# A hand-pipelined four-layer graph kernel: another order of all steps, on all engines

## The chip, the core and the metric

The kernel runs on one core of a Trainium2 chip. The core's engines work side by side: PE (TensorE, matrix products and transposes), DVE (VectorE), ACT (ScalarE), POOL (GpSimd), and SP, whose queue issues the DMA transfers. Each takes its own instructions strictly in the order in which the program gives them; an instruction whose input isn't there holds up everything behind it on its engine. The metric is the device time of one execution in microseconds (us), the median of several runs.

## What is computed

128 samples `x` of 128 nodes by 512 features, float32, go through four layers. `adj` (128 by 128) is shared by all samples. Each layer ends in `x = layernorm(x + layer(x))`.

```
layer 0:  deg = adj.sum(1);  nadj = adj * rsqrt(deg)[:,None] * rsqrt(deg)[None,:]
          nadj @ (x @ W0) + bias
layer 1:  max_j relu(A[:, j] + (C - A)[:, i]) with W1 = W2 = adj
layer 2:  q, k, v = x @ Wq.T, x @ Wk.T, x @ Wv.T
          rel = adj.T * (q @ k.T);  rel = rel / norm(rel, axis=2);  rel @ v
layer 3:  h = x @ W3;  e = leaky_relu((h @ a1)[:,None] + (h @ a2)[None,:]) * adj
          att = softmax(e);  elu(att @ h + beta * h)
```

Layer 1 adds to each row only a multiple of what the normalisation removes again, so the kernel keeps of it a factor in the variance.

## The kernel before, in words

**Tiling.** The samples are taken in 32 groups of 4; a group's `x` is one tile of 128 by 4 by 512. A program step is one small piece of one group's work, such as one product block, one copy out of PSUM, or one exchange; it is written `group.step`, as `0.w5`. Steps of the setup, common to all groups, are `s.step`.

**Order.** Three strings list the steps: HEAD (setup and the first groups), TURN (the steady state, one group per turn, with steps of five neighbouring groups mixed) and TAIL (the last groups). In TURN and TAIL the group number is relative to a base. A loop at the end of the kernel goes through HEAD, then TURN once for each group from FIRST to NG + LAST, then TAIL; `BACK` is taken off to get the base. Under `manual_schedule` the order of the steps is the order on each engine's queue. No planner intervenes afterwards. FIRST is 5 and LAST −6, so TURN is run 21 times. In TAIL the base is 22, and `9.` is the last group, 31.

**The stages of a group**, with the step names that matter here:

- `ld` loads x (`load`, L286). The loads of groups 0 to 3 and of all weights are issued once in the setup (L286, L333 to L351), in the order adj, x_0 (two halves), x_1, W0, bias, Wq, Wk, Wv, W3, a, beta, x_2, x_3.
- Layer 0: `y10 … y11` multiply nadj with x (`aggregate`, L736), ACT copies the result out of PSUM (`cy`, `copy` L375). `w1 … w7` is the product with W0 as seven blocks of Strassen's scheme (L565). Block 2 is cut again into small products (`w2`, `w28`; L529) for most groups. The left operand's sums `sy0 … sy3` run on POOL (`pool_tt`, L381). `dw`, `tw`, `uw` add the blocks into x (DVE L378, ACT L375, POOL L381), `bi` adds the bias (POOL). Then `stw` (`stats`, L770), `vaw` (L782), `pow` (POOL, L384), `nbw` (L790) and `apw` (ACT, L796) are the layernorm.
- Layer 2: `xt` transposes x on DVE in 32 by 32 blocks (`square`, L459) and `xd` completes the transposition with 16 DMAs on SP (`exchange`, L465). `sx0 … sx3` (POOL) are sums of the result, `lx1`, `lx2` sums for small blocks. `z` (with gq = Wk and Wq folded into one matrix), `r0 … r3` (`pe_r`, L905), `rm` (mask), `sq`, `rp` (norm), `rt`/`wr`/`cr` (the transposition of rel through DRAM, L497 and L501), `v` (the product with wvT) and `f`/`fa` (rel times v, L953, added on DVE at L963) follow, and the layernorm with `v`.
- Layer 3: `sc` (the two scores of every sample, DVE, L972, with `wa_bc` = W3·a spread over the partitions), `pw`/`pe` (the second score through DRAM; for the last group four PE transposes `ps`, L896), `pl`, `ej`, `ei`, `ex`, `rd`, `so` (mask and softmax), `at`/`aw`/`cat` (att transposed through DRAM; for the last group by PE, `pat`), `nt`/`nd` (x transposed and exchanged, as above), `k` (product with W3), `h` (att times it), `em`, `ee`, `ea` (elu; L1061, L1064, L1068), the layernorm with `k`, and `fin` (output DMA, L805). The last group's product is a plain one (`k_plain`, L827; half columns in `jk`, L869 to L891).

**The setup.** `s.g1 … s.g7` is the product gq (seven blocks, bank by bank), with `cg`, `dg`, `tg`, `ug` putting it together; its sums of Wq are `s.sa0 … s.sa3` on POOL, of Wk `s.sk`. `s.vt` and `s.vd` transpose and exchange Wv (16 DMAs on SP), `s.sv` are its sums. Eight `s.q` (DVE, L662) form wa = W3·a. `s.wd` (SP, L675) writes it to DRAM as `d_wa`, `s.wb` (L679) reads it back into all partitions as `a_bc`. `s.wc0` and `s.wc1` (ACT, L375) copy it to two PSUM banks kept for it. `wb` waits for `wd`, `wc` for `wb`.

**Buffers.** PSUM: 6 banks in a ring (tag "bank") and the two of `wa_bc`. Left operands aT and their sums S have 3 buffers each, most others one. The tile `q` of the small blocks, allocated in `before`, has one buffer.

Of the kernel before, what the change touches and what calls it, by code (L numbers as in the profile page):

```python
# [50 lines left out]
FIRST = 5  # L51
LAST = -6
BACK = 4
HEAD = """
s.warm s.deg s.root s.nadj s.adjt s.nadjT 0.ld 0.y10 0.y00 0.cy10 0.y11 0.cy00 0.sy1 1.ld 0.y01
0.cy11 1.y10 0.cy01 0.sy0 1.y00 1.cy10 0.sy2 1.y11 1.cy00 1.y01 1.cy11 s.s00 0.sy3 0.w1 1.cy01
s.s02 0.w5 s.s01 0.dw1 0.bi01 0.w7 0.dw5 s.sa0 s.s03 0.w2 0.dw7 s.sa1 0.w6 s.sk0 0.dw2 s.sa2
0.w3 0.tw s.sk2 s.sk1 0.w4 s.m02 0.dw3 s.sa3 s.g1 0.dw4 0.bi00 s.g2 s.cg1 s.sk3 s.vt0 0.bi10
s.g5 s.vt1 0.bi11 s.dg2 s.vt2 s.g7 s.cg5 0.uw01 s.vt3 2.ld 3.ld s.vd s.q00 s.g6 s.dg7 0.uw10
0.stw0 0.uw11 s.g3 0.stw1 s.q01 s.tg s.g4 0.stw2 1.sy0 0.stw3 1.sy1 1.w1 s.dg3 0.vaw 1.sy2 s.dg4  # L60
1.w5 1.dw1 0.pow s.q02 1.w7 0.nbw 1.dw5 1.ly2 0.apw0 0.apw1 1.dw7 0.apw2 s.q03 1.w2 0.apw3 s.q10
1.w6 1.bw2 0.xt0 1.sy3 1.ew2 s.ug11 1.w3 0.xt1 1.bi10 1.tw 0.xt2 1.w28 0.xt3 1.w4 1.bi00 0.xd
s.sg0 2.y10 s.sv0 2.y00 s.sg2 2.cy10 s.sg1 2.y11 2.cy00 s.sv2 2.cy11 s.sg3 s.sv1 1.dw3 1.bi11
1.dw2 2.y01 1.bi01 1.dw4 2.cy01 s.sv3 s.q11 s.q12 s.q13 s.s30 s.wd s.bi 1.uw01 0.z1 s.s32 1.stw0
0.sx0 0.cz1 1.stw1 0.sx1 0.z5 s.wb s.mg1 0.z2 0.cz5 s.s31 0.sx2 0.z7 0.dz2 s.mg2 s.wc0 0.z6
0.dz7 0.sx3 s.wc1 4.ld s.s33 0.z3 1.uw10 0.z4 1.uw11 2.sy0 0.tz 1.stw2 0.dz3 0.uz11 0.dz4 0.r0
1.stw3 2.sy1 0.r1 1.vaw 0.r2 1.pow 0.r3 2.ly2 0.v1 0.rm 0.rt 0.sq0 0.sq1 2.sy2 0.wr 0.v5 0.cv1
0.sq2 1.nbw s.mv1 0.sq3 1.apw0 0.v2 2.sy3 0.cv5 1.xt0 0.cr 1.apw1 0.v7 0.dv2 0.rp 1.apw2 1.xt1
2.bi10 1.apw3 1.xt2 0.v6 0.dv7 2.bi00 1.xt3 0.v3 0.tv 1.xd s.mv2 0.uv11 0.v4 0.dv3 2.bi11 0.f0
0.dv4 2.bi01 0.f1 0.fa0 0.f2 0.stv0 0.f3 0.fa1 0.fa2 3.y10 0.fa3 3.y00 3.cy10 3.bi10 0.stv1  # L70
3.y11 3.cy00 0.stv2 3.bi00 3.y01 3.cy11 0.stv3 3.sy0 2.w1 3.cy01 0.vav 0.pov 2.w5 2.dw1 3.sy1
2.w7 0.nbv 2.dw5 1.lx1 0.apv0 0.apv1 0.nt0 2.w2 0.apv2 2.dw7 1.sx0 0.nt1 2.w6 0.apv3 0.nt2 1.lx2
2.bw2 2.ew2 2.w3 2.tw 0.nt3 1.sx1 0.sc00 2.w28 1.sx2 2.dw3 2.w4 0.sc01 3.ly2 0.sc10 1.z1 0.nd
0.sc11 1.z5 1.bz1 1.sx3 0.sc20 1.ez1 3.sy2 1.z2 0.sc21 1.z18 1.bz2 2.uw01 0.sc30 1.z7 1.cz1
# [48 lines left out]
2.apk3
"""
TURN = """
4.z1 1.fin2 3.fa3 4.sx1 1.fin3 4.z5 4.bz1 3.stv0 4.sx2 4.ez1 4.z2 2.so0 3.stv1 4.z18 4.bz2 6.ld
4.ez2 4.z7 4.cz1 4.sx3 4.cz5 3.stv2 2.so1 4.z6 4.dz7 3.stv3 4.z28 4.tz 2.at 4.z3 4.uz11 4.dz2
# [98 lines left out]
9.k3 9.jc2 9.stk1 8.fin0 8.apk1 9.vak1 8.apk2 9.h2 9.pok1 8.fin1 9.nbk1 9.ck3 8.fin2 9.jk3 9.em2  # L226
8.apk3 9.ee2 8.fin3 9.apk0 9.h3 9.ea2 9.em3 9.ee3 9.fin0 9.jc3 9.stk2 9.apk1 9.j3 9.ea3 9.je3
9.fin1 9.jm3 9.stk3 9.ja3 9.vak2 9.jt3 9.pok2 9.vak3 9.nbk2 9.pok3 9.apk2 9.nbk3 9.jp3 9.apk3
9.fin2 9.fin3 9.jf3
"""  # L230


# [927 lines left out]
```

## Time and profile before

| | |
|---|---|
| median of 3 runs | 2022.46 us (2022.35 to 2023.34) |
| span of the profiled execution | 2019.7 us |
| granted PE clock, mean | 0.995 |
| instructions | 32758 |
| busy PE, DVE, POOL, ACT | 1992.9, 1645.2, 1330.2, 829.7 us |
| x load of a group, 1 MB, issue to landing (median) | 5.3 us |
| relT and attT DMAs, issue to landing (median) | 2.5 us |
| x_0T exchange, 16 DMAs: issue begins, last begins to move, p_z starts | 50.22, 60.28, 62.71 us |

The span is the time from the first to the last instruction in one profiled execution. The runs are timed apart from it and lie some us above. All figures in microseconds; "busy" is the time in which an engine works on an instruction, idle is the rest of the span. PE's granted clock is a share of full speed. The chain of waits follows the end back, at each step to what released it.

### The profile page before, as it was taken

To read this page: it belongs to the slowest core of one execution; us is meant where nothing else is said; L and a number is where in the kernel's file an instruction comes from. 1 tells how busy PE (TensorE), PEld (TensorE's weight loads), DVE (VectorE), ACT (ScalarE), POOL (GpSimd) and SP (SyncE) were. 2 spreads that over 40 slices of the span, in tenths; PEclk is the share of its full clock that TensorE was granted. 3 is DMA by queue.
4 is the path that set the end of the run, shared out by engine and by line. 5 is a ranking of instruction groups with operands and counts; after the bars stand their busy time and mean duration, and the time that the engine had idled before them with its cause. 6 is when DMAs were issued, how large, how long until landed. Compare 5 with 4: busy or idle time off the path is not lost.

```text
span 2019.7 us, 32758 instructions
## 1 busy us (share of the span) xinstructions
PE 1992.9 (99%) x10921; PEld 1715.3 (85%) x10921; DVE 1645.2 (81%) x3490; ACT 829.7 (41%) x1797; POOL 1330.2 (66%) x1429
## 2 busy tenths in 40 slices
PE   9899999999999999999999999999999999999997
PEld 8798888888888888888888888888888888888875
DVE  6878788888888888888888888888888888888886
ACT  2234334444344443444443444433444434444344
POOL 7677557766668666677666677666676668567551
PEclk9999999999999999999999999999999999999998
DMA  7433344443444444434344444444344444443443
GB/s 225 82 66 80 68 87 103 90 78 90 102 90 96 83 83 97 95 91 97 69 95 105 89 94 83 81 94 103 89 97 75 87 101 88 96 102 65 70 85 88
DMA packets 737975, 184.78 MB, mean 91 GB/s; under 512 B 689936, under 2 KB 690320, under 8 KB 737808
## 3 DMA queue, kind: packets, MB, share of 16 engines
q1 hardware_dynamic: 737664, 182.56, 41.8%
q8 instruction: 88, 1.44, 0.3%
q14 instruction: 79, 0.65, 0.1%
q10 hardware_dynamic: 144, 0.13, 0.0%
HBM read 64.55 MB, written 49.87 MB: 57 GB/s over the span
## 4 chain that ended last, share of the span: by engine, by line
PE 97%; SPq 1%; DVE 1%; DMA 0%; issue 0%; ACT 0%; POOL 0%; DVEq 0%; POOLq 0%
PE p_k L565 16%; PE p_w L565 16%; PE p_z L565 14%; PE p_v L565 13%; PE pr L905 6%; PE py L736 6%; PE pl_v L953 5%; PE pl_k L953 5%; PE p_z L529 5%; PE p_v L529 5%; PE p_k L529 2%; PE p_w L529 2%; SPq L465 1%; PE pk L827 1%; DVE e L972 0%
## 5 line engine op out<-in xcount | busy, mean ns | idle before, releaser
L796 ACT ACTIVATE x<-x,nb,r 128x512 f32<-128x512 f32 x383 | 282.5, 804 | 188.9 <-DVE nb L790 176.9
L381 POOL TENSOR_TENSOR x<-x,t_w 128x512 f32<-128x512 f32 x96 | 120.8, 1285 | 122.1 <-ACT t_w L375 122.1
L381 POOL TENSOR_TENSOR x<-x,bias_bc 128x512 f32<-128x512 f32 x128 | 162.7, 1291 | 37.1 <-PE py L736 28.9
L378 DVE TENSOR_TENSOR x<-p_w,x 128x512 f32<-128x512 f32 x192 | 129.4, 687 | 57.6 <-PE p_w L565 38.6
L972 DVE SCALAR_TENSOR_TENSOR e<-x,wa_bc 128x512 f32<-128x512 f32 x256 | 173.2, 676 | 3.8 <-ACT x L796 0.9
L384 POOL TENSOR_TENSOR r<-n,minus_half 128x4 f32<-128x4 f32 x32 | 32.4, 1012 | 174.5 <-ACT pr L920 174.5
L384 POOL TENSOR_TENSOR r<-v,minus_half 128x4 f32<-128x4 f32 (+1 forms) x99 | 98.9, 999 | 52.8 <-DVE v L782 44.4
L736 PEld LDWEIGHTS py<-nadjT,x 128*128 128x128 f32 x1024 | 120.3, 193 | 2.8 <-DVE nadjT L633 0.8
L963 DVE SCALAR_TENSOR_TENSOR x<-pl_v,r,x 128x512 f32<-128x512 f32 x128 | 90.1, 743 | 39.5 <-PE pl_v L953 38.7
L565 PE MATMUL p_z<-S_x,gq 128*128 128x256 f32 x512 | 121.2, 380 | 0.0
L565 PE MATMUL p_v<-wvT,S_x 128*128 128x256 f32 x512 | 121.1, 379 | 0.0
L565 PE MATMUL p_z<-S_x,gq_t 128*128 128x256 f32 x512 | 121.1, 379 | 0.0
L736 PE MATMUL py<-nadjT,x 128*128 128x128 f32 x1024 | 120.6, 277 | 0.4 <-DVE nadjT L633 0.4
L565 PE MATMUL p_v<-wvT_t,S_x 128*128 128x256 f32 x512 | 121.0, 379 | 0.0
L565 PE MATMUL p_w<-w_t,S_y 128*128 128x256 f32 x512 | 121.0, 379 | 0.0
L565 PE MATMUL p_w<-w,S_y 128*128 128x256 f32 x512 | 120.9, 379 | 0.0
L565 PE MATMUL p_k<-w_t,S_n 128*128 128x256 f32 x496 | 118.4, 382 | 0.0
L565 PE MATMUL p_k<-w,S_n 128*128 128x256 f32 x496 | 117.2, 379 | 0.0
L953 PE MATMUL pl_v<-C_v,relT 128*128 128x512 f32 x248 | 111.6, 592 | 0.0
L953 PE MATMUL pl_k<-C_k,attT 128*128 128x512 f32 x248 | 111.5, 592 | 0.0
L1061 DVE SCALAR_TENSOR_TENSOR x<-pl_k,x 128x512 f32<-128x512 f32 x127 | 86.8, 688 | 29.7 <-PE pl_k L953 29.4
L565 PEld LDWEIGHTS p_w<-w,S_y 128*128 128x128 f32 x512 | 97.3, 190 | 13.2
(1580 smaller groups left out, 5425.2 us busy)
## 6 DMA issues: line engine op xcount, KB each, us to landing
out_dram<-x SPq DMA_DIRECT2D x127, 256.0 KB, 2.0
x<-in_x_dram SPq DMA_DIRECT2D x31, 1024.0 KB, 5.3
d_r<-ru SPq DMA_DIRECT2D x31, 256.0 KB, 2.3
relT<-d_r SPq DMA_DIRECT2D x124, 64.0 KB, 2.5
s<-d_s SPq DMA_DIRECT2D x31, 256.0 KB, 3.7
d_a<-au SPq DMA_DIRECT2D x31, 256.0 KB, 2.0
attT<-d_a SPq DMA_DIRECT2D x124, 64.0 KB, 2.5
x<-in_x_dram SPq DMA_DIRECT2D x2, 512.0 KB, 4.4
```

The costliest lines, as they stand in the source:

```text
L378: nc.vector.tensor_tensor(o, a, b, f)
L381: nc.gpsimd.tensor_tensor(o, a, b, f)
L384: nc.gpsimd.tensor_tensor(o, v, minus_half[:, : v.shape[-1]], ALU.pow)
L529: nc.tensor.matmul(self.banks[i][:, r, bass.ts(c, P)], lhsT=lhsT, rhs=rhs, start=(not then and n == 0), stop=(n == len(steps) - 1), skip_g ...
L565: nc.tensor.matmul(ps[:, j, :], lhsT=lhsT, rhs=rhs, start=(i not in ONTO and j == 0 and kc == 0), stop=(j == 1 and kc == 1), skip_group_ch ...
L736: nc.tensor.matmul(o, lhsT=self.x_chunk(b, kc), rhs=nadjT, start=True, stop=True)
L796: nc.scalar.activation(xt, xt, AF.Identity, bias=self.nb[k][:, b : b + 1], scale=self.rstd[k][:, b : b + 1],)
L905: nc.tensor.matmul(self.pr[:, b, :], lhsT=self.whole["z"][:, fc, b // 2, bass.ts(b % 2, P)], rhs=self.xT.chunk(b, fc), start=(fc == 0), st ...
L953: nc.tensor.matmul(ps, lhsT=left[:, b, :], rhs=self.whole[k][:, b, :], start=True, stop=True)
L963: nc.vector.scalar_tensor_tensor(xt, self.pf[b], self.rnorm[:, b : b + 1], xt, ALU.mult, ALU.add)
L972: nc.vector.scalar_tensor_tensor(wide(self.e), self.x[:, b, :], 1.0, wide(wa_bc[k]), ALU.mult, ALU.mult, accum_out=self.s[:, k, b : b + 1],)
L1061: nc.vector.scalar_tensor_tensor(xt, self.pz[b], 0.0, xt, ALU.max, ALU.add)
```

## The change

Every step that the program ran before runs again, once. Their order in HEAD, TURN and TAIL is new on every engine. The counts at the top differ: HEAD now holds the beginnings of more groups (FIRST 9), TURN runs 18 times with a base of g − 3, and TAIL begins at base 24, so that `7.` in it is the last group, 31. The loop gets a STEP of 1. Since steps of a sample number b no longer come with b = 0 first, the allocations ask whether the tile is there yet instead of whether b is 0 (`square`, `room`, `pe_r`, `sq`, `sc`, `exp`, `c_plain`, `half`), the dictionaries `pf`, `pz`, `pk` are made with the group, and `q` is kept by block number.

The strings, cut to the stretches that the prediction speaks of: HEAD's start, parts of TURN, and TAIL from the last group's `sc` and `pe` on.

```diff
-FIRST = 5
-LAST = -6
-BACK = 4
+FIRST = 9
+LAST = -5
+STEP = 1
+BACK = 3
 HEAD = """
-s.warm s.deg s.root s.nadj s.adjt s.nadjT 0.ld 0.y10 0.y00 0.cy10 0.y11 0.cy00 0.sy1 1.ld 0.y01
-0.cy11 1.y10 0.cy01 0.sy0 1.y00 1.cy10 0.sy2 1.y11 1.cy00 1.y01 1.cy11 s.s00 0.sy3 0.w1 1.cy01
-s.s02 0.w5 s.s01 0.dw1 0.bi01 0.w7 0.dw5 s.sa0 s.s03 0.w2 0.dw7 s.sa1 0.w6 s.sk0 0.dw2 s.sa2
-0.w3 0.tw s.sk2 s.sk1 0.w4 s.m02 0.dw3 s.sa3 s.g1 0.dw4 0.bi00 s.g2 s.cg1 s.sk3 s.vt0 0.bi10
-s.g5 s.vt1 0.bi11 s.dg2 s.vt2 s.g7 s.cg5 0.uw01 s.vt3 2.ld 3.ld s.vd s.q00 s.g6 s.dg7 0.uw10
-0.stw0 0.uw11 s.g3 0.stw1 s.q01 s.tg s.g4 0.stw2 1.sy0 0.stw3 1.sy1 1.w1 s.dg3 0.vaw 1.sy2 s.dg4
-1.w5 1.dw1 0.pow s.q02 1.w7 0.nbw 1.dw5 1.ly2 0.apw0 0.apw1 1.dw7 0.apw2 s.q03 1.w2 0.apw3 s.q10
-1.w6 1.bw2 0.xt0 1.sy3 1.ew2 s.ug11 1.w3 0.xt1 1.bi10 1.tw 0.xt2 1.w28 0.xt3 1.w4 1.bi00 0.xd
-s.sg0 2.y10 s.sv0 2.y00 s.sg2 2.cy10 s.sg1 2.y11 2.cy00 s.sv2 2.cy11 s.sg3 s.sv1 1.dw3 1.bi11
-1.dw2 2.y01 1.bi01 1.dw4 2.cy01 s.sv3 s.q11 s.q12 s.q13 s.s30 s.wd s.bi 1.uw01 0.z1 s.s32 1.stw0
-0.sx0 0.cz1 1.stw1 0.sx1 0.z5 s.wb s.mg1 0.z2 0.cz5 s.s31 0.sx2 0.z7 0.dz2 s.mg2 s.wc0 0.z6
-0.dz7 0.sx3 s.wc1 4.ld s.s33 0.z3 1.uw10 0.z4 1.uw11 2.sy0 0.tz 1.stw2 0.dz3 0.uz11 0.dz4 0.r0
-1.stw3 2.sy1 0.r1 1.vaw 0.r2 1.pow 0.r3 2.ly2 0.v1 0.rm 0.rt 0.sq0 0.sq1 2.sy2 0.wr 0.v5 0.cv1
...
+1.ld 2.ld 0.ld s.warm s.deg 3.ld s.root s.nadj s.adjt s.nadjT 0.y10 s.s00 0.y11 0.cy10 s.sa1 s.s02
+1.y00 0.cy11 s.s01 s.sa0 1.y10 s.s03 1.cy00 s.vt0 0.sy0 1.y01 1.cy10 s.vt1 1.y11 s.vt2 1.cy01
+s.sa2 s.sk0 0.w5 1.cy11 s.vt3 1.bi10 s.sk1 s.vd s.sk2 0.y00 1.sy0 s.sk3 0.y01 0.dw5 0.cy00 s.sa3
+s.q03 2.y10 0.cy01 s.s30 0.bi01 0.w2 s.q11 s.s31 0.sy1 s.q02 0.w1 2.bi10 s.m02 s.q00 0.w7 0.sy2
+0.dw1 s.q01 1.sy2 0.w6 0.dw7 0.sy3 0.dw2 s.bi 0.w4 s.q10 0.tw 0.bi11 s.s33 s.s32 1.sy3 s.g2 s.q13
+2.cy10 0.dw4 0.uw11 s.sv0 s.g5 s.q12 0.bi10 s.sv2 s.wd 0.bi00 s.sv1 0.w3 s.cg5 s.sv3 0.uw10 s.g3
+s.wb 0.dw3 1.sy1 0.stw2 0.stw3 s.g7 0.uw01 1.ly2 0.stw0 s.g1 0.stw1 s.wc0 s.dg7 s.wc1 1.w5 0.vaw
+s.cg1 4.ld 0.pow s.dg2 0.nbw s.g4 1.dw5 0.apw0 0.apw1 0.xt0 s.g6 0.apw2 0.xt1 0.apw3 0.xt2 0.xt3
+1.w2 s.tg 0.xd s.dg3 s.ug11 1.w7 1.bw2 s.dg4 1.ew2 1.w1 1.dw7 s.sg0 1.bi11 1.w28 s.sg2 1.w4 1.dw1
+s.sg1 1.bi00 s.sg3 1.w6 1.dw4 1.dw2 1.w3 1.tw 1.uw10 2.y11 1.dw3 1.uw11 2.y00 2.cy11 1.bi01 1.stw2
+2.y01 2.cy00 1.stw3 2.w1 2.sy0 2.cy01 0.sx1 0.z1 1.uw01 0.z7 s.mg1 0.cz1 0.sx0 1.stw1 2.sy1 0.z5
+1.stw0 2.sy2 1.vaw 0.v7 0.cz5 2.ly2 0.dz7 0.z2 2.sy3 0.sx2 0.z4 0.dz2 s.mg2 2.bi01 0.v1 0.sx3 0.z6
+2.bi00 s.mv1 0.cv1 1.pow 2.dw1 0.z3 0.tz 2.bi11 1.nbw 0.dz4 1.apw3 0.v6 0.uz11 1.apw2 0.dz3 1.xt3
...
 TURN = """
-4.z1 1.fin2 3.fa3 4.sx1 1.fin3 4.z5 4.bz1 3.stv0 4.sx2 4.ez1 4.z2 2.so0 3.stv1 4.z18 4.bz2 6.ld
-4.ez2 4.z7 4.cz1 4.sx3 4.cz5 3.stv2 2.so1 4.z6 4.dz7 3.stv3 4.z28 4.tz 2.at 4.z3 4.uz11 4.dz2
...
-5.xt2 6.cy10 6.bi11 2.h0 5.xt3 6.cy11 5.xd 2.h1 6.cy01 2.em0 6.sy0 3.ex0 2.h2 2.em1 2.ee0 6.sy1
-2.h3 2.em2 2.ee1 3.ex1 2.ea0 3.k1 6.sy2 2.ee2 2.em3 3.ex2 2.ea1 6.ly2 2.ee3 3.k5 2.ea2 3.ck1
-2.ea3 3.ex3 2.stk0 6.sy3 3.k7 3.ck5 2.stk1 6.bi01 2.stk2 3.k2 3.dk7 3.k6 3.bk2 2.stk3 3.ek2 3.k3
-3.tk 3.uk11 2.vak 3.rd 3.k28 3.dk3 2.pok 3.k4 3.dk2 5.lx1 4.f0 2.nbk 4.f1 4.fa0 5.sx0 2.apk0
...
+3.w1 2.bz2 1.nt0 2.uz11 2.ez2 1.nd 2.z4 3.dw1 1.sc00 2.z28 1.sc01 3.w7 2.dz4 2.dz2 1.sc10 2.r0
+3.dw7 1.sc11 2.r1 1.sc20 2.r2 1.sc21 2.r3 1.sc30 3.w4 2.rm 1.sc31 2.sq0 2.sq1 3.w6 2.rt 2.sq2 1.pw
...
+3.nbw 0.stk2 3.apw2 2.v28 1.rd 2.uv11 3.apw0 4.y10 3.xt2 3.apw3 2.dv2 2.v4 1.so0 3.xt0 3.apw1
+3.xt3 4.cy10 4.bi10 3.xt1 4.cy11 0.h1 2.dv4 3.xd 4.sy1 1.k1 0.em1 0.ee1 4.sy0 0.ea1 0.h3 4.bi11
+0.stk1 1.k2 1.ck1 0.em3 1.k6 4.sy2 1.bk2 0.ee3 1.ek2 4.ly2 1.k5 0.ea3 1.tk 0.stk3 4.sy3 0.vak
...
+2.fa3 3.sx0 2.fa2 3.z1 2.fa1 3.sx1 5.ld 4.w5 3.bz1 2.stv2 3.sx2 3.ez1 3.z5 2.stv1 3.sx3 4.dw5 1.h0
+2.stv3 3.cz5 3.z18 1.em0 3.z3 2.vav 3.cz1 2.pov 1.ee0 1.ea0 3.z6 2.nbv 1.stk0 2.apv1 2.apv3 2.nt1
+3.z7 3.tz 2.nt3 2.apv2 3.dz3 2.apv0 2.nt2 3.z2 3.dz7
...
 TAIL = """
...
-7.uk11 9.nt1 7.k28 9.apv3 7.dk3 7.k4 8.ex0 7.dk2 8.ex1 9.nt2 8.ex2 7.h0 7.dk4 8.ex3 7.h1 9.nt3
-8.rd 9.nd 7.h2 7.em0 8.so0 7.em1 7.ee0 7.h3 7.em2 8.so1 7.ee1 7.em3 7.ee2 8.at 7.ee3 7.ea0
-9.sc00 7.ea1 9.sc01 9.sc10 9.sc11 9.sc20 9.sc21 9.sc30 8.aw 9.sc31 7.ea2 9.pe 8.k1 9.pl0 7.ea3
-9.pl1 7.stk0 9.pl2 9.pl3 8.cat 7.stk1 8.k5 8.ck1 9.ej 7.stk2 9.ei 8.k7 8.ck5 7.stk3 9.ex0 9.ex1
-7.vak 8.k2 8.dk7 7.pok 9.ex2 9.ex3 8.k6 7.nbk 8.bk2 9.rd 9.so0 7.apk0 8.ek2 7.apk1 7.fin0 8.k3
-9.so1 8.tk 7.fin1 9.so2 7.apk2 9.so3 8.uk11 8.k28 8.dk3 7.apk3 7.fin2 8.k4 8.dk2 7.fin3 8.h0
-8.dk4 9.rb 8.h1 8.h2 8.em0 8.em1 8.ee0 8.h3 8.em2 8.ee1 9.at 8.em3 9.k0 8.ee2 9.cat 8.ee3 8.ea0
-8.ea1 8.ea2 8.ea3 9.k1 9.ck0 8.stk0 8.stk1 9.h0 9.ck1 8.stk2 9.jk1 9.em0 8.stk3 9.ee0 9.k2 9.jc1
-9.ea0 8.vak 9.stk0 8.pok 9.h1 9.ck2 9.vak0 9.pok0 9.jk2 9.em1 8.nbk 9.ee1 9.nbk0 8.apk0 9.ea1
-9.k3 9.jc2 9.stk1 8.fin0 8.apk1 9.vak1 8.apk2 9.h2 9.pok1 8.fin1 9.nbk1 9.ck3 8.fin2 9.jk3 9.em2
...
+7.dv2 7.f2 6.pw 7.fa3 7.f0 7.stv3 7.f1 7.fa2 6.sn1 6.pe 7.fa0 5.k5 7.fa1 6.sn0 7.stv0 5.k1 6.ln2
+5.ck5 7.stv1 5.dk7 6.pl1 7.stv2 5.k2 6.sn2 6.pl2 5.ck1 5.k4 6.pl0 7.vav 5.bk2 7.pov 6.pl3 5.ek2
+6.sn3 5.k6 7.nbv 7.apv0 6.ej 7.apv2 7.nt0 5.k3 7.apv1 7.nt2 7.apv3 6.ei 7.nt1 5.k28 5.tk 6.ex2
+7.nt3 5.uk11 6.k7 6.ex1 5.dk2 7.nd 6.ex3 5.dk4 6.ex0 5.dk3 6.k2 6.rd 6.so0 5.h2 7.rb 6.bk2 5.h0
+6.so1 5.em2 5.h3 6.ek2 5.ee2 6.k1 5.ea2 5.em0 6.at 5.ee0 6.k28 5.em3 6.k5 7.sc00 5.ee3 5.ea0
+7.sc01 5.h1 5.stk0 6.ck5 7.sc10 6.ck1 6.k3 6.aw 5.em1 7.sc11 5.ee1 6.dk7 6.k6 7.sc20 5.ea1 6.k4
+7.sc21 6.tk 6.cat 6.uk11 5.stk1 6.dk2 7.jk1 6.dk4 7.sc30 7.k1 6.dk3 7.sc31 5.ea3 7.pe 5.stk2 6.h3
+7.pl1 7.pl0 5.stk3 7.pl2 6.h1 7.pl3 6.em3 7.ej 6.h2 6.em1 6.ee3 6.h0 5.vak 6.ee1 6.em2 5.pok 7.ei
...
 """
...
         def square(self, b, x):
-            if b == 0:
+            if not hasattr(self, "u"):
...
-            self.banks = {}
+            self.banks, self.q = {}, {}
...
         def before(self, i):
-            self.q = mid.tile([P, 2, P], F32, tag="q", name=f"q_{self.name}")
-            copy(wide(self.q), wide(self.banks[i])[:, 0 : 2 * P])
+            q = self.q[i] = mid.tile([P, 2, P], F32, tag="q", name=f"q{i}_{self.name}")
+            copy(wide(q), wide(self.banks[i])[:, 0 : 2 * P])
...
         def pe_r(self, b):
-            if b == 0:
+            if not hasattr(self, "pr"):
...
         for base, steps in (
-            [(0, HEAD)] + [(g - BACK, TURN) for g in range(FIRST, end)] + [(end - BACK, TAIL)]
+            [(0, HEAD)] + [(g - BACK, TURN) for g in range(FIRST, end, STEP)] + [(end - BACK, TAIL)]
         ):
```

## Prediction, made before the run

> **What bounds the kernel now.** I read five views, from coarse to fine. First the page: the engine totals, the span in 40 slices and the chain that ended last.
>
> ```profile
> span 2019.7 us, 32758 instructions
> PE 1992.9 (99%) x10921; PEld 1715.3 (85%) x10921; DVE 1645.2 (81%) x3490; ACT 829.7 (41%) x1797; POOL 1330.2 (66%) x1429
> PE   9899999999999999999999999999999999999997
> PE 97%; SPq 1%; DVE 1%; DMA 0%; issue 0%; ACT 0%; POOL 0%; DVEq 0%; POOLq 0%
> ```
>
> PE carries 97% of the chain; only the second and the last slice show a hole. A busy PE is not yet a PE at its own rate, so next the chain in order of time:
>
> ```profile
> 50.22 0.58 SPq L465
> 60.28 2.08 DMA x_0T<-sq_x
> 62.71 14.00 PE p_z L565 x56
> 80.47 12.09 PE p_v L565 x56
> ...
> 1274.52 5.18 PE p_w L565 x24
> 1335.90 5.18 PE p_w L565 x24
> 1947.60 3.70 PE pl_v L953 x8
> 1975.30 8.09 PE p_k L565 x24
> ```
>
> The same piece returns after 1335.90 − 1274.52 = 61.38 us: one group. The chain's `p_w x24` gives a pitch of 5.18/24 = 0.216 us for a 256-column matmul pass, `py x32` 3.57/32 = 0.1116 for a 128-column one, and `pl_k x8` 3.44/8 = 0.43 for 512. One group issues (two-digit blocks are the small ones) y 3.57, w 10.36+1.56, z 9.53+2.23, r 3.57, v 9.53+2.23, f 3.44, k 10.36+1.56, h 3.44: sum 61.4. So the middle runs at PE's own rate, and the order of work in it has nothing to give. Summing every PE step of the whole program this way gives 1980.0 us, the same for both versions. All that an order can win or lose is 2019.7 − 1980.0 = **39.7 us**. The waits say where it lies:
>
> ```profile
> PE p_z L565 <- DMA x_0T<-sq_x: 8.1, 1, 8.1
> PE ps L896 <- DVE e L972: 6.9, 4, 3.9
> PE pz L869 <- ACT C_k_end L375: 1.2, 1, 1.2
> PE pl_v L953 <- ACT relT_end L375: 0.7, 1, 0.7
> 58.00:60.00 2.00, 0.00 (x0) 0.00 (x0) 1.93 (x7) 0.00 (x0) 0.00 (x0) 0.82 0.60 89
> 64.00:66.00 2.00, 2.00 (x6) 1.53 (x6) 1.70 (x3) 0.00 (x0) 2.00 (x2) 0.50 0.00 0
> ```
>
> Columns of the first four: total us, times, longest. In the last two (stretches): after the length, PE, PEld, DVE, ACT, POOL, then the granted clock. After the long wait the clock is 0.50, and `p_z x56` takes 14.00 where `p_v x56` takes 12.09: 1.9 us more. My account of the 39.7: start 17.8 (5.6 before the first y, 1.45 of half clock, small waits 0.8, the 8.1, the 1.9), middle about 1.2 (no PE wait is listed between 80 and 1940 us), tail 20.4: relT 0.85, four waits of `ps` with the hand-over between them 8.2, half clock after them 2.9 (8.09 − 5.18), `pz` 1.45, and 7.0 from the last matmul to the end.
>
> **What the Trainium skill says.** "TensorE: Matmul & The Clock Gate", HAM oscillation: PE idle for over about 3.4 us falls to half clock. The trace agrees: 0.50 after the 8.1 us wait. "DMA: Bandwidth & Descriptors", Two DMAs through the same engine are not ordered: a DMA that reads what another writes must wait for its semaphore. So `d_wa<-wa`, then `a_bc<-d_wa`, cost two landings in series; the trace has 69.59 − 61.01 = 8.6 and 5.1. "SBUF — State Buffer", Who interferes with whom: VectorE with two SBUF inputs contends with GpSimd's reads. That fits POOL's sums here (1.24 to 1.75 us for one form) but no run isolates it.
>
> **The change, part by part.** No step is added or removed: 7062 steps, the same in both, in another order. The allocation guards and the dictionaries for q issue nothing: 0. STEP=1 changes nothing either (the loop before already had step 1). Three parts remain.
>
> *Start: +8.5 us.* I follow the built order against landing times (issue plus landing: wq 16.3, wv 22.2, a 26.3, x_2 29.0, x_3 31.7).
> 1. POOL now has two wq sums ahead of group 0's first S_y. They wait for 16.3, take 2.95 (as in the timeline before), and S_y 1.5 more. PE's 0.w5 waits for it, to about 20.9, at half clock; before, S_y began at 9.51.
> 2. PE's 2.y10 stands ahead of 0.w2, w1, w7, w6, w4 and waits for x_2: 29.0 to 29.4, with 8.9 us of work done. Lag 20.2 to 20.5; before, PE was done with all of 0.w at 26.3. The idle before it is under 3.5 us, so I count no second clock loss.
> 3. SP's wvT exchange: seven DMAs early, the eighth behind x_3's slot at 31.7, nine at 0.67 and landing 2.3: 39.9. Then DVE's sv0 and the last s.q: `wa` is ready at 41.4, d_wa issued at 42.
> 4. 42 + 8 = 50 (d_wa), + 5.1 = 55.2 (a_bc). On ACT the two `wa_bc` copies (1.11) now stand **ahead** of cg1 (the gq copy) and of 0.apw0 to 3. Queued behind them: cg1, four applies. PE's g6 waits for cg1 and DVE's dg2 too, ahead of 0.nbw. PE stops at 52.4 to 52.9 with 32.2 done and restarts at 57.2: lag 25. Before, these copies waited 5.97 us on an ACT with nothing urgent behind.
> 5. 0.apw0 to 3 end at 61.0, the last transpose at 61.6, the x exchange is issued at 61.9 (4.ld is already past it in SP's queue), and 12.5 us after its start (50.22 to 62.71 before) 0.z1 starts at 74.5 to 74.8. PE has 48.5 done: lag 26.3 against 17.8. **+8.5**, ends +2.7 (d_wa lands in 3 us, as `d_s`, 1.4 to 4.7) and +10.5 (the clock falls at g6 as well).
>
> *Head and turns: +2.7.* A turn is a permutation of the same 61.4 us of PE. Followed step by step, the nearest supplies to PE are: z3 (from the x exchange and four POOL sums at 1.24) 0.3 us early, z5 and r0 0.8, v18 1.1, h0 1.2. In before the exchange had some 5 us to spare. With 0.3 us of cover I take 0.2 us lost in each of 18 turns, 3.6, and 0.3 in HEAD, minus the 1.2 of before: **+2.7**; ends −1.2 (none) and +17 (chain 1 us longer: 0.7 × 23 groups, +0.3).
>
> *Tail: −9.6.* The last group's 31.pe stands now after 30.k and 29.h: with 1961.9 us of work done, not 1946.5. So `s` has 15.4 us more. But DVE must finish the same eight sc (0.73 each), with the elu of 29 and 30 between; by my count it ends about 0.5 to 1 us after PE arrives. After the last matmul I count 9 us (before 7.0), as the last pieces run through elu, statistics, pow and apply later. Now 0.8 + 1.0 (the attention transposes) + 9.0 = 10.8 against 20.4: **−9.6**; no clock loss, since no wait reaches 3 us. Ends −11 and −2 (`ps` again late by 4 us, half clock with it).
>
> Sum: +8.5 + 2.7 − 9.6 = **+1.6 us** against the span 2019.7, so 2021.3; the median of the runs, 2022.46, lies 2.8 above the span, so **2024 us**.
>
> **The rivals.**
> A. *The start costs little.* `d_wa` lands in 3 us: then a_bc arrives by 50, before PE stops, the exchange starts 5.8 us sooner, and the sum is +1.6 − 5.8 = −4.2: **2018**; with turns without a stall, 2014. For it: before, the write was issued right behind sixteen exchange DMAs. Against: its 4 KB are 1024 pieces of 4 B, and the DMA engines show 0.00 in 64 to 66 us, so it wasn't waiting for data ahead of it.
> B. *The turn's x exchange binds* (slower). Place: TURN, xt, xd, four POOL sums, z3. It decides from 0.3 us on; at 1 us over, 0.7 us × 23 = 16.1 in place of 3.6: +1.6 + 12.5 = +14.1, **2037**. For it: the smallest slack of all, and POOL's sums vary by 0.5 us. Against: every landing of the exchange was 2.3.
> C. *DVE binds in the tail.* DVE is near full there by my count (busy 47.91 of 61.00 in 1952 to 2013 before), so `ps` waits 4 us and the clock falls: +1.6 + 7.6 = **2032**.
> D. *The change isn't what it says*: "one group, not three" isn't seen in the code before, whose turn is one group. So no gain can come from it; its effect is within the forecast.
>
> **How the numbers follow.** What a measurement can tell from no change is 0.2%, 4 us. Forecast 0.49 (own range 2018 to 2030: faster 0.06, same 0.29, slower 0.14), A 0.26 (faster 0.23, same 0.03), B 0.15 (slower), C 0.10 (slower 0.09, same 0.01). Faster 0.29, same 0.33, slower 0.38. The range that leaves out 2 in 10 runs from 2013 to 2037.
>
> **What would show it.** Right: PE waits of 0.w5 on POOL, `py` on DMA x_2 near 29 us, `p_g` on ACT's gq copy near 57 with ACT waiting for a_bc just before; z1 near 74.8; the same 61.38 period; `ps` waiting under 1 us; 8 to 10 us from the last matmul to the end. Wrong: z1 before 70 us (A), a period above 61.8 (B), `ps` over 3 us (C). A PE total other than 1980 at full clock would overturn the whole frame.

## The result, and the profile after

| | before | changed |
|---|---|---|
| median | 2022.4 us (2020.71 to 2023.34, 4 runs) | 2051.87 us (2049.16 to 2056.02, 4 runs) |
| ratio | | 1.0149, interval [1.0135, 1.0163] |
| span of the profiled execution | 2019.7 | 2051.9 |

The changed kernel is slower, by about 30 us; 2024 was predicted, with 2013 to 2037. First the same parts of its page:

```profile
span 2051.9 us, 32535 instructions
...
PE 2010.7 (98%) x10921; PEld 1719.6 (84%) x10921; DVE 1679.3 (82%) x3490; ACT 830.0 (40%) x1797; POOL 1331.1 (65%) x1429
...
PE   7899999999999999999999999999999999999997
...
PE 70%; DVE 9%; SPq 7%; POOL 6%; DMA 5%; issue 2%; ACT 1%; POOLq 0%; DVEq 0%; ACTq 0%
```

The work is the same: as many matmuls, and POOL as busy to 1 us. But PE carries 70% of the chain that ended last, where it carried 97%; DVE, POOL, SP's queue and DMAs have the rest. DVE is busy 34 us longer with the same 3490 instructions, so some of them take longer than they did. Next PE's waits (total us, times, longest):

```profile
PE p_w L598 <- POOL S_y L419: 6.4, 1, 6.4
PE p_g L598 <- ACT gq L413: 4.1, 1, 4.1
PE py L770 <- DMA x<-in_x_dram: 2.9, 2, 1.9
PE p_z L598 <- POOL S_x L419: 2.6, 7, 0.5
PE pl_v L986 <- DVE C_z L416: 2.6, 1, 2.6
PE p_w L598 <- DVE x L416: 2.3, 1, 2.3
PE p_g L598 <- DVE gq L416: 1.9, 1, 1.9
```

The first three are the waits that the prediction's start named. The long `ps` wait of the tail is gone.

To see where each microsecond enters I take PE's **lag**: the start of a matmul less the time that all matmuls before it take at full clock (0.111, 0.216 and 0.43 us for 128, 256 and 512 columns; 1979.8 us in all). It grows by waits and by half clock, and can't shrink. "z0" is group 0's first product of layer 2, "w9" and "w27" are the layer 0 block `w1` of groups 9 and 27. A lag is of the one profiled execution of its kernel; the four runs of the changed kernel spread over 7 us, so a difference of one or two microseconds between totals shows nothing.

| lag, us | z0 starts | at z0 | at w9 | at w27 | at the end | head | turns | tail |
|---|---|---|---|---|---|---|---|---|
| before | 62.7 | 15.9 | 18.3 | 18.7 | 39.9 | 2.4 | 0.4 | 21.3 |
| changed | 84.1 | 35.6 | 48.5 | 57.5 | 72.1 | 12.9 | 9.0 | 14.6 |

"Head" is w9 less z0, "turns" w27 less w9, "tail" the rest. The 32.2 us between the spans are +19.7 up to z0, +10.5 in the head, +8.6 in the turns and −6.7 in the tail. (Before, 1.9 of the head's 2.4 is half clock right behind z0's wait, which the prediction counted to the start.) In the prediction's own terms the lags were to be 26.3 at z0, 0.3 in the head, 3.6 in the turns and 10.8 in the tail; they were 35.6, 12.9, 9.0 and 14.6. The largest miss is the head.

### The profile page after: what moved, and what is told of

Its sections match the earlier page's. It is cut to its first block, busy times and chain, and to the rows that moved or that the text cites. A ratio compares the mean times of both kernels' runs of the same rounds, so it can differ in the third digit from the quotient of the medians.

```text
span 2051.9 us, 32535 instructions
## 1 busy us (share of the span) xinstructions
PE 2010.7 (98%) x10921; PEld 1719.6 (84%) x10921; DVE 1679.3 (82%) x3490; ACT 830.0 (40%) x1797; POOL 1331.1 (65%) x1429
## 4 chain that ended last, share of the span: by engine, by line
PE 70%; DVE 9%; SPq 7%; POOL 6%; DMA 5%; issue 2%; ACT 1%; POOLq 0%; DVEq 0%; ACTq 0%
PE p_w L598 12%; PE p_z L598 11%; PE p_k L598 10%; PE p_v L598 10%; SPq L503 7%; PE pr L938 4%; PE py L770 4%; PE pl_k L986 4%; PE pl_v L986 4%; PE p_z L562 3%; PE p_v L562 3%; PE p_w L562 2%; POOL S_x L419 2%; POOL L_x L419 2%; PE p_k L562 1%
## 5 line engine op out<-in xcount | busy, mean ns | idle before, releaser
L419 POOL TENSOR_TENSOR x<-x,bias_bc 128x512 f32<-128x512 f32 x128 | 164.5, 1289 | 57.5 <-PE py L770 41.5
L770 PEld LDWEIGHTS py<-nadjT,x 128*128 128x128 f32 x1024 | 129.0, 196 | 17.1 <-issue 11.2
L770 PE MATMUL py<-nadjT,x 128*128 128x128 f32 x1024 | 132.7, 279 | 3.3 <-DMA x<-in_x_dram 2.9
L419 POOL TENSOR_TENSOR C_z<-C_z,t_z 128x512 f32<-128x512 f32 x32 | 40.7, 1271 | 139.8 <-DVE C_z L416 129.1
L953 ACT ACTIVATE pr<-rel 128x128 f32<-128x128 f32 x128 | 36.0, 281 | 231.0 <-DVE rel L416 228.1
L986 PE MATMUL pl_k<-C_k,attT 128*128 128x512 f32 x248 | 125.7, 594 | 1.6 <-DVE x L1099 0.6
L598 PEld LDWEIGHTS p_w<-w_t,S_y 128*128 128x128 f32 x512 | 96.5, 194 | 21.9 <-POOL S_y L419 6.6
```

What stands on the lines that cost most here:

```text
L419: nc.gpsimd.tensor_tensor(o, a, b, f)
L598: nc.tensor.matmul(ps[:, j, :], lhsT=lhsT, rhs=rhs, start=(i not in ONTO and j == 0 and kc == 0), stop=(j == 1 and kc == 1), skip_group_ch ...
L770: nc.tensor.matmul(o, lhsT=self.x_chunk(b, kc), rhs=nadjT, start=True, stop=True)
L986: nc.tensor.matmul(ps, lhsT=left[:, b, :], rhs=self.whole[k][:, b, :], start=True, stop=True)
```

## The experiments

### Does DVE wait for POOL?

Kernel `m_lock` does none of the reference's work. It puts rows of equal operations on DVE and POOL beside each other (`tt` is DVE, `ptt` POOL; `bank` lies in PSUM, the other operands in SBUF):

```python
"two": lambda: tt(od, a, b, ALU.add),
"psum": lambda: tt(od, a, bank, ALU.add),
"tiny": lambda: nc.vector.scalar_tensor_tensor(small_d, a[:, 0:GB], -1.0, b[:, 0:GB], ALU.mult, ALU.mult),
...
"sum": lambda: ptt(op, c, d, ALU.add),
```

> Computes nothing of the reference: it copies the first four samples to all of the output and times DVE and POOL operations in fourteen stretches, alone and side by side. Theory 1 (a DVE operation with two SBUF inputs and a POOL sum hold the same port and take turns, each for its whole length): DVE adds of 128x512 from two SBUF tiles, 0.6 us apart alone, come 1.7 to 1.9 us apart beside POOL sums, and the sums 1.7 to 1.9 instead of 1.25; a DVE add with one input in PSUM stays at 0.6 and POOL at 1.25; DVE's 128x4 operations of the layernorm, 0.15 us alone, are 1.2 us apart. Rival (DVE is only slower in the setup because of the loads that run there): every DVE operation keeps its pace beside POOL's sums, within 10%.

From the timelines of DVE and POOL (start, busy time of the row in us, then the operation and the count):

```profile
6.95 8.68 DVE L97 TENSOR_TENSOR od<-xs 128x512 f32<-128x512 f32 x12
...
15.91 12.93 POOL L106 TENSOR_TENSOR op<-xs 128x512 f32<-128x512 f32 x8
16.07 20.14 DVE L97 TENSOR_TENSOR od<-xs 128x512 f32<-128x512 f32 x12
...
46.99 17.28 DVE L98 TENSOR_TENSOR od<-xs,bank 128x512 f32<-128x512 f32 x24
64.25 2.33 DVE L99 SCALAR_TENSOR_TENSOR small_d<-xs 128x4 f32<-128x4 f32 x12
66.61 9.79 DVE L99 SCALAR_TENSOR_TENSOR small_d<-xs 128x4 f32<-128x4 f32 x16
```

An addition of two SBUF inputs takes 8.68/12 = 0.72 us with POOL idle and 20.14/12 = 1.68 beside POOL's sums, which take 12.93/8 = 1.62 there (1.7 to 1.9 was expected). With one input in PSUM it stays at 17.28/24 = 0.72 beside the sums. A 128x4 operation goes from 0.19 to 0.61 (1.2 was expected, so that size was wrong). That is what the Trainium skill, "SBUF — State Buffer", Who interferes with whom, states in words: a DVE instruction with two SBUF inputs contends with POOL's reads. The prediction cited this and gave it no price; the price is a factor of 2.3. Below I call this the lock.

### The start: three mends

The kernel `e_wc` moves the copies that stood ahead of the gq copy on ACT:

```diff
-... s.g1 0.stw1 s.wc0 s.dg7 s.wc1 1.w5 0.vaw s.cg1 4.ld 0.pow ... 0.xd s.dg3
+... s.g1 0.stw1 s.dg7 1.w5 0.vaw s.cg1 0.pow ... 0.xd s.wc0 s.wc1 4.ld s.dg3
```

> The changed kernel with the two copies of a_bc into PSUM (and the load of group 4, which needs a_bc's buffer) behind the x exchange of group 0. Theory 1 of the start (ACT's in-order wait for a_bc holds up the gq copy and the applies): PE's wait of 4.1 us for the gq copy and the half clock behind it go, group 0's first z product starts 5 to 7 us sooner than 84.1 us, and the whole is 4 to 6 us shorter, about 2046. Rival (SP's wait for d_wa, which stands ahead of the x exchange, takes its place, or PE is held by DVE's gq additions): z starts within 1.5 us of 84.1 and the time stays within 2 us of 2051.9.

z0 started at 77.24, 6.9 us sooner, and the wait for the gq copy was gone. At the end less was left, 3.3 us by the medians where 4 to 6 were expected: 2048.61 us (2046.08 to 2050.49), ratio 1.0137 [1.0123, 1.015].

`e_qp` takes the lock off the eight `s.q`: `a` is copied into the two PSUM banks first (two more copies on ACT, not shown), and the products read it there.

```diff
-                a_bc[:, k, :],
+                wide(wa_bc[k]),
```

> The changed kernel with the vector a copied by ACT into the two PSUM banks early, so that the eight s.q products of DVE read one input from PSUM and one from SBUF; two copies of 0.58 us are added. Theory 1 (in the setup DVE waits for POOL's sums, since both inputs of s.q are in SBUF): the s.q take 0.7 us each in place of 1.3 on average, d_wa is issued 4 to 6 us sooner than 49.26, PE's wait for the gq copy shrinks from 4.1 us to under 1, and the whole is 3 to 6 us shorter, about 2047. Rival (DVE has too much work in the setup, whoever runs beside it): d_wa within 1.5 us of 49.26, no gain.

Each `s.q` took 0.67 us (1.28 in the mean in the changed kernel), `d_wa` was issued at 45.03 in place of 49.26, z0 started 5.6 us sooner. PE's wait for the gq copy, which was to shrink to under 1 us, stayed at 4.1; the wait of 2.3 us for DVE at 39 us went down to 0.6. But the head then lost 14.1 and the tail 15.9: 2051.61 us (2050.23 to 2055.68), 1.0153 [1.0137, 1.0168], no gain that can be told from none.

`h_start` takes the whole start back: the order of before up to its step 0.z6, then the changed order for what remains.

> The kernel before up to group 0's block 6 of the z product (step 173 of 7062), and from there the changed order, as far as its steps are not done yet. If the start alone costs what the two traces show (35.6 us of PE idle and slow clock up to the first z product against 15.9, and 1.9 more just behind it), the whole is 15 to 19 us shorter than the changed kernel, 2033 to 2037, and the later losses (12.9 us from there to group 9's w product, 8.9 in the turns) stay. Rival (the later losses are the start's consequence and go with it): under 2025.

2041.38 us (2039.03 to 2042.84), 1.0095 [1.0078, 1.0112]. The lag at z0 was 15.7, so 19.9 us were won there; half came out (10.5 by the medians, where 15 to 19 were expected), because the head lost 17.8 and the turns 12.7. Neither theory of that expectation held: the later losses did not stay, and did not go; they grew. What made the head lose 4.9 more was not taken apart.

### The turns: late exchanges and POOL's queue

In the changed TURN the work between the landing of the x exchange and the last S_x sum is all POOL's, and POOL is ready as soon as it lands. `e_lx2` moves one set of small sums behind the four S_x:

```diff
-... 3.lx1 2.f0 1.dk4 2.f3 2.fa0 3.lx2 1.cat ... 3.z5 2.stv1 3.sx3 4.dw5
+... 3.lx1 2.f0 1.dk4 2.f3 2.fa0 1.cat ... 3.z5 2.stv1 3.sx3 3.lx2 4.dw5
```

> The changed kernel with POOL's second set of small sums (lx2, four of 0.46 us, needed by z's last small product only) put behind the four large sums sx0 to sx3 in TURN and TAIL. If z waits for POOL's sums behind the x exchange (rival B of the prediction), the waits of z for S_x go and the 18 turns lose 5 to 6 us in place of 8.9. If the turn is held by POOL's queue as a whole or by DVE's operations beside it, nothing is gained: 8 to 9.5 us.

PE's waits for S_x in the turns are gone, and the turns lost 6.2 in place of 9.0; 2049.69 us (2047.77 to 2052.12), 1.014 [1.0125, 1.0155], which can't be told from the changed kernel.

`e_nobi` leaves out the bias additions, four sums per group on POOL:

```diff
         def bias(self, p, h):
+            return
```

> The changed kernel without the addition of the bias (128 POOL additions of 1.29 us; nothing is put in their place). If POOL's queue is what makes the changed order late (its sums stand behind the exchange, and it holds the port that DVE wants), the turns go back to 61.4 to 61.5 us, the stretch from the first z product to group 9's w product loses at most 7 us instead of 12.9, and the whole is 12 to 20 us shorter. If the DMA exchange, ACT or DVE's own work sets it, the turns stay at 61.8 and the gain is under 4 us, from the start alone.

The waits for S_x are gone here too. The turns lost 3.3 and the head 9.0 (7 at most was expected). The total came out 10 us shorter, where 12 to 20 were expected: 2041.81 us (2040.49 to 2042.77), 1.01 [1.0085, 1.0115].

> The changed order without the bias additions (left out: x + bias in layer 0, four of POOL's sums per group), and with lx2 behind the four S_x sums in TURN and TAIL. Alone the first gave turns of 3.3 us lost in place of 9.0, the second 6.2. Theory 'POOL's queue behind the x exchange is all that the turns lose': together the turns lose under 1.5 us, the total is 2 us or more under that without the bias alone (2041.8). Rival 'something else holds the turn as well': still 2.5 us or more, the total within 1.5 us of 2041.8.

The two together: 2042.54 us (2040.9 to 2043.27), 1.0097 [1.008, 1.0114], the turns lost 4.3. No more than the bias alone gives, so the rival in that expectation held: some 2 to 3 us of the turns are not the work that was taken from POOL there. A part can be read off: every turn of the changed order loses at least 0.14 us, without a wait (0.03 in before), 2.0 us more in 18 turns.

The opposite edit, `e_nbp`, takes small operations from DVE (`va`, `nb` of every layernorm, which the lock stretches) and gives them to POOL:

```diff
-                nc.vector.tensor_scalar(v, var, EPS, None, ALU.add)
+                nc.gpsimd.tensor_scalar(v, var, EPS, None, ALU.add)
...
-            nc.vector.scalar_tensor_tensor(
-                self.nb[k][:, b], self.mv[k][:, b, 0], -1.0, self.rstd[k][:, b], ALU.mult, ALU.mult
...
+            nc.gpsimd.tensor_scalar(self.nb[k][:, b], self.mv[k][:, b, 0], -1.0, None, ALU.mult)
...
+            pool_tt(self.nb[k][:, b], self.nb[k][:, b], self.rstd[k][:, b], ALU.mult)
```

> The changed kernel with the layernorm's two small DVE operations per group and layer (variance plus eps, minus mean times r) done by POOL around its pow. Theory 1 (each small DVE operation waits for POOL's running sum, on the way from the statistics to the apply, the transposes and the exchange): the turns go back from 61.9 us on average to 61.4 to 61.5, and the stretch from group 9's to group 27's first w product loses at most 2 us instead of 8.9; the whole is 6 to 12 us shorter, about 2043. Rival (the exchange with its sixteen DMAs and POOL's four sums is too long by itself, and the new POOL operations make POOL later still): the turns stay at 61.8 or more and the time is 2050 or more.

2069.22 us (2066.98 to 2070.27), 1.0238 [1.0224, 1.0252]: 17 us slower than the changed kernel where 6 to 12 faster was expected. Of this, 10.1 us lie in the head, 5.8 in the tail and 2.7 in the turns. PE's wait for S_x became 5.4 us in 12 waits (2.6 in 7). My theory of that moment, that the late small DVE operations hold the turn, fell. That POOL's queue does, and that these operations lengthened it, fits `e_nobi`, but this edit alone doesn't separate it.

`h_turn` asks whether the turns lose only because the head hands over late.

```diff
-order = changed HEAD, changed TURN x18, changed TAIL
+order = steps of before up to 8.k28, then the changed order's steps that are left
```

> The order of before up to its step 8.k28 (group 8's layer 3, where the two orders differ by three steps only), then the changed order's turns and tail. PE comes to the turns some 18 to 21 us behind its own work, not 48. Theory 'the changed turn has a longer period of its own': the turns from group 9 to 27 lose at least the 9.0 us that they lose in the changed kernel, and as in h_start (12.7) rather more; with the tail of h_tail, 2016.7 + 9 to 14 = 2026 to 2031. Rival 'the turns lose only because HEAD hands over late': they lose under 3 us, and the total is 2016 to 2020.

2027.52 us (2023.39 to 2029.33), 1.0022 [1.0013, 1.0031]. With the start and head of before the turns still lost 12.0, so the loss is their own. `h_tail` below has the turns of before and the same tail, and is 10.9 us faster. PE's waits in `h_turn`:

```profile
PE p_z L860 <- DMA x_0T<-sq_x: 8.1, 1, 8.1
PE p_z L860 <- POOL S_x L681: 3.5, 9, 0.9
```

What decides a turn is seen turn by turn. In SP's queue, two turns of before and two of the changed kernel (start and length of the sixteen issues):

```profile
811.03 11.22 SPq L465 DMA_DIRECT2D x_13T<-sq_x  x16
...
872.41 12.01 SPq L465 DMA_DIRECT2D x_14T<-sq_x  x16
```

```profile
1092.55 10.70 SPq L503 DMA_DIRECT2D x_17T<-sq_x  x16
...
1154.05 11.62 SPq L503 DMA_DIRECT2D x_18T<-sq_x  x16
```

In both kernels some exchanges take longer than the usual 10.70 us to issue; in the changed one x_26T also took 2.9 in place of 1.5 us to land after its last issue. After x_14T, 1.3 us late, before lost nothing: POOL had other work until then, and in groups 10 to 27 of before it never stood idle for the landing by more than 0.07 us. In the changed order it stood idle for it in every one of these turns, 0.7 to 2.4 us. After x_18T, 0.9 us late, POOL does this:

```profile
1167.28 0.87 POOL L419 TENSOR_TENSOR L_x<-x_18T 128x128 f32<-128x128 f32 x2 [1.68 <-DMA x_18T<-sq_x]
...
1170.83 2.50 POOL L419 TENSOR_TENSOR S_x<-x_18T 128x512 f32<-128x512 f32 x2
...
1174.64 1.27 POOL L419 TENSOR_TENSOR S_x<-x_18T,S_x 128x512 f32<-128x512 f32 x1
```

POOL stood idle 1.68 us for the landing, then has 3.6 us of L_x and 5.1 of S_x; its last sum ends at 1175.91 and PE's product of it starts at 1175.96. In a turn whose exchange is on time that margin is 0.2 to 0.6 us. In this turn PE lost 0.10 us at that product, and 0.33 shortly before it at the product that takes attT. SP issues attT behind the exchange; it landed at 1174.23 and PE went on at 1174.32, where in the turn before PE began 1.5 us after the landing. The larger loss, 0.6 us, came 30 us later at another hand-over. ACT's copy C_v stands behind four operations that wait for the second score, which comes back from DRAM, and PE waits for the copy:

```profile
1202.38 1.80 ACT L1030 ACTIVATE e<-s,s 128x128 f32<-128x128 f32 x4 [1.50 <-DMA s<-d_s]
1204.09 0.56 ACT L413 COPY C_v<-p_v 128x512 f32<-128x512 f32 x1
1204.71 1.99 PE L598 MATMUL p_v<-wvT_t,S_x 128*128 128x256 f32 x8 [0.33 <-ACT C_v L413]
```

Counting a turn as late when first issue to last landing took over 0.15 us more than the usual 12.17, and its loss as the growth of the lag from one group's z to the next (groups 10 to 27):

| | late turns | lag they lost, us | of it where z waits for S_x | other turns | lag they lost, us |
|---|---|---|---|---|---|
| before | 8 | 0.2 | 0 | 10 | 0.2 |
| changed | 6 | 6.5 | 2.8 | 12 | 2.8 |
| h_turn | 8 | 10.1 | 5.9 | 10 | 2.2 |
| e_m32 (below) | 8 | 10.4 | 6.0 | 10 | 2.7 |
| e_lx2 | 7 | 2.7 | 0 | 11 | 3.3 |
| e_nobi | 6 | 1.1 | 0 | 12 | 2.3 |

Late exchanges are as frequent in before, and cost it nothing. In the changed order a turn with one loses 1.1 to 1.3 us, 0.5 to 0.75 of it where z waits for S_x; where POOL has less to do ahead of the last sum, that part is gone and a late turn loses a sixth to a third. Of what is left, 1.9 us in the late turns of the changed kernel is the wait for C_v, and 1.2 in those of `e_lx2`. That it follows from the late exchange isn't shown: `e_lx2` loses another 1.0 there in turns whose exchange is on time.

Nor is the lateness spread evenly. In these six traces the exchanges of groups 10, 14, 18, 22 and 26 are late in 27 of 30 cases, those of the other 13 groups in 16 of 78.

### The head, and all mends together

At 177 us DVE does four small sums of a W3 block, `s.m32`, in the middle of POOL's sums, and the copy that PE waits for stands behind them. In the changed kernel, and in `e_m32`, which moves the step 25 places later, to where POOL is idle:

```profile
177.11 0.73 DVE L365 TENSOR_TENSOR m<-w 128x128 f32<-128x128 f32 x1
177.88 1.01 DVE L365 TENSOR_TENSOR m<-w,m 128x128 f32<-128x128 f32 x1
178.82 1.35 DVE L365 TENSOR_TENSOR w<-w 128x128 f32<-128x128 f32 x1
180.10 1.35 DVE L365 TENSOR_TENSOR m<-w,m 128x128 f32<-128x128 f32 x1
...
182.98 0.66 DVE L416 TENSOR_TENSOR C_z<-p_z,t_z 128x512 f32<-128x512 f32 x1
```

```profile
188.36 0.26 DVE L363 TENSOR_TENSOR m<-w 128x128 f32<-128x128 f32 x1
188.66 0.29 DVE L363 TENSOR_TENSOR m<-w,m 128x128 f32<-128x128 f32 x1
188.86 0.28 DVE L363 TENSOR_TENSOR w<-w 128x128 f32<-128x128 f32 x1
189.07 0.28 DVE L363 TENSOR_TENSOR m<-w,m 128x128 f32<-128x128 f32 x1
```

```diff
-... 3.dw4 2.z6 s.m32 0.so0 3.stw2 ... 1.fa3 1.stv3 0.k7
+... 3.dw4 2.z6 0.so0 3.stw2 ... 1.fa3 1.stv3 s.m32 0.k7
```

> The changed order with one step of HEAD moved: s.m32 (the four small sums of a block of W3, on DVE, 4 us beside POOL's sums at 177 to 181 us) stands 25 steps later, behind 1.stv3, where DVE is idle. Theory 'HEAD has single late hand-overs': the wait of pl_v for DVE (2.6 us at 183.7) and the half clock after it (about 1.5) go, head 12.9 -> about 9, and the total is 3 to 4 us under the changed kernel's. Rival 'the order downstream runs at a pace of its own': the wait goes, but the head or the turns lose as much again by group 27, and the total moves by less than 1.5 us.

The same four additions take 1.1 us, not 4.4 (the lock in the kernel itself), the wait of `pl_v` and the half clock behind it are gone, and the head lost 8.5, not 12.9. But the turns lost 13.0 in that execution, and its late turns, eight and not six, account for 3.9 of the 4.0 us more: 2050.38 us (2049.69 to 2052.69), 1.0139 [1.0124, 1.0154]. By the medians 1.5 us of 4.4 were kept, which can't be told from none, as the rival in that expectation had it. Why the number of late exchanges differs from trace to trace is open.

> The changed order with four mends together: the copies s.wc0, s.wc1 and 4.ld behind 0.xd, the s.q products reading a_bc from PSUM, lx2 behind the S_x sums, s.m32 later. Alone they gave 3.3, 0, 2.2 and (this batch) some 3 us. Theory 'one thing after another decides, each mend uncovers the next': less than the start's gain of 10 us or more arrives at the end; 2037 to 2044. Rival 'the mends add up, and the order is as good as the old one without them': 2028 to 2034. Neither gets under the kernel before, whose turns lose 0.4.

The four mends together (`e_wc`, `e_qp`, `e_lx2`, `e_m32`): 2037.94 us (2037.65 to 2040.39), 1.0078 [1.0063, 1.0093]; lag at z0 25.0, head 8.4, turns 5.8, tail 16.9. The total is in the expected range, but not for the reason given there: the start's 10.6 us did arrive; 14 us in all. The order still lies 15 above before.

### The tail, and a version that beats both

> The kernel before up to group 26's block 2 of the k product (step 6140 of 7062), and from there the order of the changed kernel, as far as its steps are not done yet. If the changed tail is worth what its trace shows (14.6 us from the last full turn to the end against 21.2), the whole is 5 to 8 us shorter than before, 2014 to 2017. Rival (the gain comes only because the changed kernel is late elsewhere, and its other engines have caught up): within 2 us of 2022.4.

`h_tail` is the order of before up to its step 26.k2, then the changed order. It took **2016.67 us** (2014.36 to 2017.74, 13 runs), ratio 0.9974 [0.9966, 0.9983] to before: head 2.4 and turns 0.4 as in before, tail 14.5 as in the changed kernel. It beats both. Most of the gain is the wait of `ps`, which no longer shows: the last group's scores on DVE have more time.

## Why the prediction was wrong

**Start, steps 1 and 2: right.** PE waited for S_y to 20.50 (about 20.9 predicted), and 2.y10 started at 29.01 (29.0).

**The clock in step 2: wrong.** At 29.01 the lag was 20.2, as step 2 had it. It said "The idle before it is under 3.5 us, so I count no second clock loss". PE's timeline:

```profile
29.01 1.44 PE L770 MATMUL py<-nadjT,x 128*128 128x128 f32 x8 [1.93 <-DMA x<-in_x_dram]
...
39.28 3.13 PE L598 MATMUL p_w<-w_t,S_y 128*128 128x256 f32 x8 [2.28 <-DVE x L416]
```

and stretches of it (length; PE, PEld, DVE, ACT and POOL busy; granted clock; DMA share; GB/s):

```profile
28.00:29.00 1.00, 0.00 (x0) 0.02 (x1) 1.00 (x2) 0.00 (x0) 1.00 (x2) 1.00 1.05 387
29.00:33.00 4.00, 3.99 (x15) 3.46 (x16) 4.00 (x6) 0.00 (x0) 3.82 (x3) 0.58 1.17 192
...
33.00:39.00 6.00, 4.00 (x19) 3.17 (x17) 5.97 (x10) 0.00 (x0) 4.04 (x3) 0.99 0.65 98
39.00:43.00 4.00, 3.72 (x10) 3.01 (x11) 4.00 (x7) 0.55 (x1) 2.49 (x2) 0.61 0.23 36
...
64.80:70.00 5.20, 5.18 (x16) 4.47 (x17) 4.88 (x9) 3.51 (x5) 0.64 (x1) 0.50 0.61 205
```

The clock was full again (1.00 and 0.99) before each of these idle times, of only 1.93 and 2.28 us, and after them it fell to 0.50 for 3.4 us each; the 0.58 and 0.61 are means of the stretches. Eight products took 3.13 us where 1.73 is full speed. The 3.4 us of idle time that the Trainium skill names ("TensorE: Matmul & The Clock Gate", HAM oscillation) was no limit here. Nor does the length of one idle time decide: after another of 1.95 us, before 58.69, the clock stayed at 1.00. What decides was not tried.

From 20.2 at 29.01 the lag grew to the 35.6 at z0 by 3.7 us of slow products behind these two idle times, 2.3 and 2.1 in two waits for DVE's sums (at 39.28 and 58.69) that the prediction's walk didn't have, 4.4 at the gq copy (4.5 predicted) and 3.0 of half clock behind that, which the prediction had only as an upper end.

**Steps 3 and 4: mechanism right, size wrong.** `wa` was to be ready at 41.4; `d_wa` was issued at 49.26. The step left DVE 1.5 us for `sv0` and the last `s.q`, as if its list before them were done by 39.9. But beside POOL's sums the operations of that list take turns with the sums (DVE's begin at 30.82, 32.50 and 34.16, POOL's at 31.98 and 33.65), and the last `s.q` began at 47.47:

```profile
29.15 1.74 DVE L353 TENSOR_TENSOR w_t<-w 128x512 f32<-128x512 f32 x1
30.82 1.75 DVE L695 SCALAR_TENSOR_TENSOR wprod<-w,a_bc 128x512 f32<-128x512 f32 x1
...
37.84 0.68 DVE L695 SCALAR_TENSOR_TENSOR wprod<-w,a_bc 128x512 f32<-128x512 f32 x1
```

One product takes 1.75 us while POOL sums and 0.68 while it doesn't. Taking the lock off the products alone brought `d_wa` forward by 4.2 of the 7.9 us (`e_qp`); the rest wasn't separated. The two landings were 8.70 and 5.14 us (8 and 5.1 predicted), and the stop of `p_g` behind the copies came as described, to 64.8 and not 57.2:

```profile
63.15 1.11 ACT L413 COPY wa_bc<-a_bc 128x512 f32<-128x512 f32 x2 [14.41 <-DMA a_bc<-d_wa]
64.19 0.58 ACT L413 COPY gq<-p_g 128x512 f32<-128x512 f32 x1
```

The gq copy needed nothing from a_bc; PE had done its product by 55.0. It began only when the two copies ahead of it on ACT had waited 14.41 us and run.

**Step 5** follows: z0 at 84.1, not 74.8, lag 35.6, not 26.3. Rival A was wrong in the other direction.

**Head: 0.3 predicted, 12.9 measured.** This is the largest failed term: the prediction gives "0.3 in HEAD" with no walk through it and no reason. 4.4 us of it is `s.m32`, DVE additions that the lock stretches and the half clock behind PE's wait for them (shown); 3.9 goes when the bias leaves POOL's queue (shown, though the two may overlap). From 350 us on some 6 us come in losses under 1 us, each for another copy or sum; these weren't tested one by one, and their cause stays open.

**Turns: 3.6 predicted, 9.0 measured.** The place was right, "z3 (from the x exchange and four POOL sums at 1.24) 0.3 us early", and rival B is a part of what happened: 3.2 of the 9.0 us were lost where z waits for S_x, where B named 16.1. The term that failed was 0.2 us per turn, which came to 0.5: it took the exchange as constant ("every landing of the exchange was 2.3"). The trace before already held delays up to 1.4 us; they cost nothing there, so no list of waits showed them. The second hand-over, the copy C_v behind the score on ACT (1.9 us and more), was not on the prediction's list of near supplies.

**Tail: −9.6 predicted, −6.7 measured.** The last matmul stood 9.1 us before the end (9 predicted), and `ps` didn't wait. The 2.9 us between are hand-overs in the last groups that weren't separated.

**C** didn't happen: PE didn't wait for `ps`. **D** was right that no gain would come from there, and not that the effect lies within the forecast: an order that gives PE the same work with less margin costs time.

## What to carry to other kernels

When an order of steps is changed, compare the margins, not only the waits: list for each hand-over how early its input is, and how much its producer varies in the trace, hidden delays included; a turn with 0.4 us of margin pays for every transfer that is later than that. Durations from one profile are not constants of an operation where two engines hold each other up: price a DVE operation with two SBUF inputs at the longer time wherever POOL works beside it. Take over a new order in parts: here the new tail on the old turns was the fastest.

## What the runs showed of the hardware

- DVE with two SBUF inputs, 128x512: 0.72 us alone, 1.68 beside POOL's sums (`m_lock`). With one input in PSUM: 0.72 beside the sums. The 128x4 operation: 0.19 alone and 0.61 beside them.
- PE's granted clock fell from full to 0.50 after idle times of 1.93 and 2.28 us within the changed kernel's start, and not after one of 1.95 us there.
- Of the exchanges of sixteen DMAs, about every second or third was 0.2 to 1.9 us late in the six kernels of the table, before too, and nearly always those of groups 10, 14, 18, 22 and 26. The cause wasn't tried.
